# Graph attention and ternary FFN on one core: weight inspection as ScalarE sums during attention and wo, and a buffer of its own for every piece of the output

## Chip, cores and metric

The kernel runs on one core of one Trainium2 chip. The metric is the device time of one execution in microseconds, as the median of several runs. Lower is better.

## The reference

One layer of graph attention and one feed-forward block act on `x`, 384 nodes by 1024 features in fp32, both with a residual connection.

```
h  = layernorm(x)
q, k, v    = h @ wq.T + bq, h @ wk.T + bk, h @ wv.T + bv           # 1024 -> 1024
q2, k2, v2 = q @ wiq.T + biq, k @ wik.T + bik, v @ wiv.T + biv     # 16 heads of 64
mask[src, dst] = softplus(edge_type_weights)[type - 1], else -inf  # 12288 edges; diagonal filled
x = x + softmax(q2 @ k2.T / 8 + mask) @ v2 @ wo.T + bo
h = layernorm(x)
h = silu((h @ w1.T) * w1_s) * ((h @ w2.T) * w2_s)                  # 1024 -> 512
h = gelu((h @ h1.T) * h1_s);  h = gelu((h @ h2.T) * h2_s)          # 512 -> 512
x = x + (h @ w3.T) * w3_s                                          # 512 -> 1024
```

The five weight matrices of the feed-forward block (w1, w2, h1, h2, w3) hold only -1, 0 and 1 in these inputs.

## The kernel before

**Tiling.** The 384 nodes are three row tiles of 128 (`NT`), the 1024 features eight column tiles (`KF`). Weights come as halves of 2 MB from a pool of four buffers (`load_w`, `prefetch`), on SP's DMA queue in order; the FFN's weights in the rounded type fp32r come on POOL's queue.

**Order.** SP, ScalarE (ACT), VectorE (DVE) and TensorE run in the order in which the code is written. The stages follow one another: layernorm and transposes; the projections q, q2, v, v2, k (`project`, L143 and L152); attention; the product with wo (L423) with its layernorm; the FFN. In the first half POOL scatters the mask's 12288 values into a table in HBM with indirect DMAs (L353) and reads the table back as `nmask`.

**Attention.** There are 24 units (eight pairs of heads by three row tiles) in 13 slots: one unit in the first and the last slot, two in each other. A slot computes the scores on TensorE (`sc`, L460), adds the mask and takes the minimum on DVE (L474), and takes the exps with their sums on ACT (L476). Then it transposes the attention weights of the slot before on TensorE (`pp`, L492), which one copy on DVE (L530) and one on ACT (L531) evict, and normalises its own on DVE (L482, L484). The rest of the k2 projection (L444) is spread over the slots. After every third unit of a pair `weighted` computes the pair's output (L501) and ACT copies it into `aT` (L504).

**The inspection.** The FFN has two branches. The fast one multiplies in fp32r and is exact only when the weights need few mantissa bits; the exact one uses fp32. The kernel decides on the chip. `inspect` loads the weights in 16 pieces of 512 KB (`raw`) on SP's queue, and DVE ORs both halves of each piece into `bits` (L182), two instructions a piece. Eight pieces are looked at in k (through the two `stage` buffers), two at the end of attention plus three in a "trio" buffer of tag "t" ahead of wo, and three more in wo after row tile 0. `gather_bits` then folds the 512 columns to one by nine halving ORs (L592), masks the low 12 bits (L593) and converts (L595). In row tile 2 a matmul with `ones` sums this over the partitions (`fl`, L607), DVE copies it to the integer `flag` (L609), the engines load it into a register (`values_load`, L613), and they branch on it at the FFN (`rest`).

**wo and its layernorm.** For each row tile and half, `multiply_out` finishes an accumulation on TensorE, and `add_out` adds it to `xs` (L584) and takes its statistics (L113) on DVE. `layernorm` takes the aggregate (L122), a square root on ACT (`sd`, L124), the scales (L126, L128) and normalises one half on DVE (L134) and one on ACT (L136). `transpose_x2` (L572) turns a normalised row tile through PSUM into `x2`, with a cast on ACT (L574) and a subtraction on DVE (L565). That of row tile 0 stands behind row tile 1's layernorm, and that of tile 1 between tile 2's two halves, behind the `fl` matmul.

**The output.** The last product (L644) gives seven pieces: five of 128x512 and two of 128x256. DVE multiplies each by the scale (L725) and adds the residual (L726), and SP sends it to HBM (L727). A piece lives in one of the two buffers of tag "stage".

**The tag "t".** It has two buffers, which are taken in turn by qT, vT, kT, pTa, the trios of `raw`, and the FFN's hidden layers `g`.

Of the kernel before, what the change touches and what calls it, by code (L numbers as in the profile page):

```python
# [8 lines left out]
FP = mybir.dt.float32  # L9
FR = mybir.dt.float32r  # L10
BF = mybir.dt.bfloat16
HF = mybir.dt.float16
I32 = mybir.dt.int32
AF = mybir.ActivationFunctionType
ALU = mybir.AluOpType

N = 384
F = 1024
FH = 512
# [3 lines left out]
P = 128  # L23
NT = N // P
# [16 lines left out]
def gnn_ffn_kernel(ctx: ExitStack, tc: tile.TileContext, x, edges, etw, vecs, rows,  # L41
# [4 lines left out]
    nc = tc.nc  # L46
# [14 lines left out]
    xs = act.tile([P, NT, F], FP, name="xs")  # L61
# [103 lines left out]
    def prefetch(between=None):  # L165
        if plan:
# [2 lines left out]
    prefetch(load_small)  # L169


    bits = const.tile([P, FH], I32, name="bits")
    pieces = [(w, i) for w in (w1, w2, h1, h2, w3)
              for i in range(w.shape[0] * w.shape[1] // (P * F))]

    def inspect(raws):
        for raw in raws:
            w, i = pieces.pop(0)
            nc.sync.dma_start(raw, bass.AP(tensor=w.tensor, offset=w.offset + i * P * F,
                                           ap=[[F, P], [1, F]]))  # L180
            for h in range(2):
                nc.vector.tensor_tensor(bits, bits, raw[:, h * FH:(h + 1) * FH].bitcast(I32),  # L182
                                        op=ALU.bitwise_or)


    q2T = act.tile([P, KF, N], FP, name="q2T")
# [4 lines left out]
    with tc.tile_pool(name="edge", bufs=1) as ep, tc.tile_pool(name="krow", bufs=2) as krp, \  # L191
# [180 lines left out]
            if c0 in (2 * CHUNK, 5 * CHUNK):  # L372
                prefetch()
        load_rows()
        nc.vector.memset(bits, 0)
        read = nc.gpsimd.dma_start(nmask, cells).ins
        for i in sent[-DEEP:]:
            after(read, i)
# [26 lines left out]
        for t in range(NT):  # L405
            tc.keep_in_program_order(
                nc.gpsimd.tensor_add(xs[:, t, :], xs[:, t, :], row[:, 1, :]))
        inspect([stage.tile([P, F], FP, tag="stage", name="raw") for _ in range(8)])
        kT = project(xT, "kT", vec[:, BK:])


# [21 lines left out]
    with tc.tile_pool(name="attn", bufs=1) as ap, \  # L433
# [85 lines left out]
        for s, new in enumerate(slots):  # L519
# [7 lines left out]
            for i in range(2):  # L527
# [6 lines left out]
                if i == 0:  # L534
# [4 lines left out]
                    if s >= len(slots) - 2:  # L539
# [1 line left out]
                            begun.append((bank(), 0))  # L541
                        ps, k = begun.pop()
                        begun.append((ps, out_steps(ps, 0, 0, k, k + 3)))
        inspect_more(False, 2)
        out_steps(begun[0][0], 0, 0, KF - 2, KF - 1)
        begun = [(begun[0][0], KF - 1), (bank(), KF - 1)]
        out_steps(begun[1][0], 0, 1, 0, KF - 2)
# [36 lines left out]
        nc.vector.tensor_add(xs[:, t, c], ps, xs[:, t, c])  # L584
        statistics(t, st, half)

    def gather_bits():

        n = FH
        while n > 1:  # L590
            n //= 2
            nc.vector.tensor_tensor(bits[:, :n], bits[:, :n], bits[:, n:2 * n], op=ALU.bitwise_or)  # L592
        nc.vector.tensor_single_scalar(bits[:, 0:1], bits[:, 0:1], 0xFFF, op=ALU.bitwise_and)  # L593
        bitf = small.tile([P, 1], FP, name="bitf")
        nc.vector.tensor_copy(bitf, bits[:, 0:1])  # L595
        return bitf


    inspect_more(True)
    for t in range(NT):  # L600
        st = small.tile([P, 2, 6], FP, name="st")
        add_out(multiply_out(t, 0), t, 0, st)
        if t == 1:
            bitf = gather_bits()
        elif t == 2:
            fl = ps_mm.tile([P, 512], FP, tag="mm", name="fl")
            nc.tensor.matmul(fl[:1, :1], lhsT=bitf, rhs=ones, start=True, stop=True)  # L607
            flag = const.tile([1, 1], I32, name="flag")
            nc.vector.tensor_copy(flag, fl[:1, :1])  # L609
            transpose_x2(1)  # L610
        ps = multiply_out(t, 1)
        if t == 2:
            low_bits = nc.values_load(flag[0:1, 0:1], min_val=0, max_val=P * 0xFFF)  # L613
        add_out(ps, t, 1, st)
        layernorm(t, xn[:, t, :], st)
        if t == 0:
            inspect_more(True)
            assert not pieces
        elif t == 1:
            transpose_x2(0)  # L620


    def rest(fast):

        parts = range(2 if fast else 1)

        def mm_T(ps, todo, o, rows):

            for n, (w, x, k) in enumerate(todo):
                nc.tensor.matmul(ps[:, rows], lhsT=w[:, k, o * P:(o + 1) * P], rhs=x[:, k, rows],  # L632
                                 start=n == 0, stop=n == len(todo) - 1)

        def products(w, src):
            return [(w, src[i], k) for i in parts for k in range(w.shape[1])]

        def accumulate(groups, nk):

            for k in range(nk):  # L640
                for ps, operands in groups:
                    for i in parts:
                        l, r = operands(i, k)
                        nc.tensor.matmul(ps, lhsT=l, rhs=r, start=(i, k) == (0, 0),  # L644
                                         stop=(i, k) == (len(parts) - 1, nk - 1))

        taken = []

        def bank():
            taken.append(len(taken) % 3)  # L650
            if taken[-1] == 2:
                return ps_mm.tile([P, 512], FP, tag="mm", name="ps")
            return ps_ff.tile([P, 512], FP, tag="ff", name="ps")

        if not fast:
            plan.extend(ffn)
            for _ in ffn:
                prefetch()
            (w1s,), (w2s,), h12, (w3s,) = [queue.pop(0) for _ in ffn]
            transpose_x2(NT - 1)  # L660
            x2T = [act.tile([P, KF, N], FP, tag="xT", name="x2T")]
            nc.vector.tensor_add(x2T[0], x2[0].bitcast(FP), x2[1].bitcast(FP))
        else:
            (w1s,), (w2s,) = early
            h12, (w3s,) = [load_w(*p, rounded=True) for p in ffn[2:]]
            x2T = x2

        def hidden():
            a = act.tile([P, KF, N], FR if fast else FP, tag="t", name="g", bufs=2)
            return [a[:, i * KH:(i + 1) * KH, :] for i in parts]  # L670

        g = hidden()

        order_ff = [(o, w) for o in range(KH) for w in (w1s, w2s)]
        ahead = {}
        if fast:
            two, one = slice(0, 2 * P), slice(2 * P, N)
            for n, (o, w) in enumerate(order_ff[:3]):
                if n == 2:
                    transpose_x2(NT - 1)  # L680
                ahead[o, id(w)] = bank()
                mm_T(ahead[o, id(w)], products(w, x2T), o, two)
        for o in range(KH):
            ps = []
            for w in (w1s, w2s):
                p = ahead.get((o, id(w)))
                if p is None:
                    p = bank()
                    mm_T(p, products(w, x2T), o, slice(0, N))
                else:  # L690
                    mm_T(p, products(w, x2T), o, one)
                ps.append(p[:, :N])
            sl = stage.tile([P, N], FP, tag="sl", name="sl")
            nc.scalar.activation(sl, ps[0], AF.Silu, scale=vec[:, W1S + o:W1S + o + 1])
            full = stage.tile([P, N], FP, tag="gf", name="gf") if fast else g[0][:, o, :]
            nc.vector.scalar_tensor_tensor(full, ps[1], vec[:, W2S + o:W2S + o + 1], sl,
                                           op0=ALU.mult, op1=ALU.mult)
            if fast:
                nc.scalar.copy(g[0][:, o, :], full)
                remainder(g[1][:, o, :], full, g[0][:, o, :])  # L700

        for w, s in zip(h12, (H1S, H2S)):
            g2 = hidden()
            for some in (range(3), range(3, KH)):
                ps = [(bank()[:, :N], lambda i, k, o=o: (w[:, k, o * P:(o + 1) * P], g[i][:, k, :]))
                      for o in some]
                accumulate(ps, KH)
                for o, (p, _) in zip(some, ps):
                    full = stage.tile([P, N], FP, tag="gf", name="gf") if fast else g2[0][:, o, :]
                    nc.scalar.activation(full, p, AF.Gelu, scale=vec[:, s + o:s + o + 1])  # L710
                    if fast:
                        nc.vector.tensor_copy(g2[0][:, o, :], full)
                        remainder(g2[1][:, o, :], full, g2[0][:, o, :])
            g = g2
        half = FH // 2
        ends = [(t, a, a + FH) for t in range(NT) for a in (0, FH)][:-1]
        ends += [(NT - 1, FH, FH + half), (NT - 1, FH + half, F)]
        for some in (ends[:3], *([e] for e in ends[3:])):
            ps = [(bank()[:, :b - a], lambda i, k, t=t, a=a, b=b: (
                g[i][:, k, t * P:(t + 1) * P], w3s[:, k, a:b])) for t, a, b in some]  # L720
            accumulate(ps, KH)
            for (t, a, b), (p, _) in zip(some, ps):
                y = stage.tile([P, FH], FP, tag="stage", name="y")
                n = b - a
                nc.vector.tensor_mul(y[:, :n], p, row[:, 2, a:b])  # L725
                nc.vector.tensor_add(y[:, :n], y[:, :n], xs[:, t, a:b])  # L726
                nc.sync.dma_start(out[t * P:(t + 1) * P, a:b], y[:, :n])  # L727

    with tc.If(low_bits == 0, preferred_fallthrough_block=True) as exact:
        rest(True)  # L730
# [36 lines left out]
```

## Time and profile before

| | us |
|---|---|
| median of 3 runs (417.29 to 417.43) | 417.33 |
| the profiled execution | 417.94 |
| its span in the profile | 416.2 |
| TensorE (PE) busy | 401.9 |
| VectorE busy | 175.9 |
| ScalarE busy | 97.4 |
| GpSimd (POOL) busy | 110.3 |
| `bits` ORs of L182 (32 x 691 ns) | 22.1 |

The span is the time from the first to the last thing in the trace of one execution; the execution takes 1.74 us more than its span. Busy times are read by engine: an engine with idle time can take more work, if the idle time lies where the work is put. Stretches of the run: k from 178 to 220 us, attention from 235 to about 316, wo to 358, the FFN's first layer to 384, then its two hidden layers to 396 and the last product with the output from 396 to the end. Rows of a timeline give start, duration, engine, line, operation, what it writes and reads and, in brackets, how long the engine had been idle and what ended that.

### The profile page before, as it was taken

How to read it: one execution, taken by the hardware profiler on the slowest of the kernel's cores; microseconds unless marked ns; L12 is line 12 of the kernel's file. 1: busy time of each engine (PE TensorE's matmuls, PEld its weight loads, DVE VectorE, ACT ScalarE, POOL GpSimd, SP SyncE). 2: the span in 40 equal slices, each digit the busy share in tenths (PEclk: the TensorE clock that was granted, in tenths of full speed). 3: DMA queues.
4: the chain of work that ended last, by engine and by line, in shares of the span. 5: the costliest groups of instructions: out<-in, count | busy, mean ns of one | idle time of the engine just before them, and what ended most of it. 6: DMA issues, size and time to landing. Idle time of an engine off the chain costs nothing.

```text
span 416.2 us, 4309 instructions
## 1 busy us (share of the span) xinstructions
PE 401.9 (97%) x1549; PEld 243.2 (58%) x1549; DVE 175.9 (42%) x567; ACT 97.4 (23%) x217; POOL 110.3 (27%) x117
## 2 busy tenths in 40 slices
PE   7899999999999999999999999999999999999991
PEld 6555555555555444455555555555544444799881
DVE  5646859800000001005500177676764487321464
ACT  4511111111111000001112255655651213221410
POOL 3022435323647374744453710000000000200000
PEclk9999999999999999999999999999999999999996
DMA  7699665899050606075727242000094000740012
GB/s 269 213 334 261 200 217 149 306 388 337 2 202 1 202 2 202 0 259 198 254 100 284 77 112 90 2 0 2 2 354 152 0 0 2 240 165 0 2 50 104
DMA packets 29207, 59.64 MB, mean 143 GB/s; under 512 B 4384, under 2 KB 7296, under 8 KB 29056
## 3 DMA queue, kind: packets, MB, share of 16 engines
q1 hardware_dynamic: 22016, 49.89, 35.5%
q0 software_dynamic: 6880, 9.03, 7.6%
q10 hardware_dynamic: 288, 0.41, 0.3%
q8 instruction: 14, 0.23, 0.2%
q14 instruction: 9, 0.07, 0.1%
HBM read 57.06 MB, written 2.26 MB: 143 GB/s over the span
## 4 chain that ended last, share of the span: by engine, by line
PE 87%; DVE 6%; DMA 3%; ACT 2%; issue 1%; SPq 0%; DVEq 0%; ACTq 0%
PE ps L143 40%; PE ps L152 10%; PE ps L444 10%; PE ps L423 6%; PE ps L632 6%; PE av L501 4%; PE sc L460 4%; PE pp L492 4%; PE ps L644 3%; DMA out<-y 2%; DMA xs<-in_x 1%; DVE st L113 1%; DVE bits L182 1%; DVE y L725 1%; DVE xs L584 1%
## 5 line engine op out<-in xcount | busy, mean ns | idle before, releaser
L353 POOL DMA_INDIRECT tab<-val,cell x96 | 94.8, 987 | 126.3 <-DMA tab<-val,cell 82.8
L337 DVE SCALAR_TENSOR_TENSOR jk<-kr,key,later 128x256 bf16<-128x256 f32 x96 | 39.9, 480 | 16.6 <-DMA kr<-keyd 16.6
L444 PE MATMUL ps<-kT,wik 128*128 128x384 f32 x128 | 43.4, 487 | 0.0
L402 DVE TENSOR_TENSOR v<-ps,row 128x512 f32<-128x512 f32 x6 | 4.2, 692 | 92.4 <-PE ps L152 92.4
L423 PE MATMUL ps<-wo,aT 128*128 128x512 f32 x96 | 42.5, 593 | 0.0
L143 PE MATMUL ps<-xT,wq 128*128 128x384 f32 x128 | 41.5, 487 | 0.3 <-ACT xT L257 0.3
L143 PE MATMUL ps<-qT,wiq 128*128 128x384 f32 x128 | 41.4, 486 | 0.0
L143 PE MATMUL ps<-xT,wv 128*128 128x384 f32 x128 | 41.4, 486 | 0.0
L143 PE MATMUL ps<-xT,wk 128*128 128x384 f32 x128 | 41.4, 486 | 0.0
L152 PE MATMUL ps<-wiv,vT 128*128 128x512 f32 x96 | 41.4, 592 | 0.0
L474 DVE CUSTOM_DVE_ANT_0 e<-sc,nmask 128x384 f32<-128x384 f32 x48 | 23.9, 553 | 31.1 <-PE sc L460 31.1
L143 PEld LDWEIGHTS ps<-xT,wk 128*128 128x128 f32 x128 | 24.3, 190 | 17.2 <-issue 0.5
L143 PEld LDWEIGHTS ps<-xT,wq 128*128 128x128 f32 x128 | 24.2, 190 | 17.2 <-ACT xT L257 0.5
L143 PEld LDWEIGHTS ps<-qT,wiq 128*128 128x128 f32 x128 | 24.3, 190 | 17.0
L143 PEld LDWEIGHTS ps<-xT,wv 128*128 128x128 f32 x128 | 24.3, 190 | 17.0
L476 ACT ACTIVATE e<-e,lo 128x384 f32<-128x384 f32 x48 | 28.9, 604 | 18.5 <-DVE lo L474 18.5
L444 PEld LDWEIGHTS ps<-kT,wik 128*128 128x128 f32 x128 | 23.5, 190 | 14.6 <-ACT k2T L447 0.5
L152 PEld LDWEIGHTS ps<-wiv,vT 128*128 128x128 f32 x96 | 18.2, 190 | 22.7 <-issue 22.5
L182 DVE TENSOR_TENSOR bits<-bits,raw 128x512 int32<-128x512 int32 x32 | 22.1, 691 | 18.5 <-DMA raw<-in_w 17.7
L423 PEld LDWEIGHTS ps<-wo,aT 128*128 128x128 f32 x96 | 17.7, 190 | 20.2 <-issue 20.2
L632 PE MATMUL ps<-x,w 128*128 128x384 f32 (+2 forms) x176 | 25.8, 306 | 0.0
L632 PEld LDWEIGHTS ps<-x,w 128*128 128x128 f32 x176 | 25.1, 190 | 0.5 <-issue 0.5
(113 smaller groups left out, 353.5 us busy)
## 6 DMA issues: line engine op xcount, KB each, us to landing
kr<-keyd SPq DMA_DIRECT2D x11, 576.0 KB, 6.5
raw<-in_w SPq DMA_DIRECT2D x12, 512.0 KB, 4.5
w<-in_w POOLq DMA_DIRECT2D x3, 2048.0 KB, 10.7
wiq<-in_wiq SPq DMA_DIRECT2D x2, 2048.0 KB, 14.9
wv<-in_wv SPq DMA_DIRECT2D x2, 2048.0 KB, 15.8
wiv<-in_wiv SPq DMA_DIRECT2D x2, 2048.0 KB, 16.1
wk<-in_wk SPq DMA_DIRECT2D x2, 2048.0 KB, 8.5
wik<-in_wik SPq DMA_DIRECT2D x2, 2048.0 KB, 8.1
```

Source lines behind the costliest of these rows:

```text
L143: nc.tensor.matmul(ps[:, :N], lhsT=w[:, k, o * P:(o + 1) * P], rhs=src[:, k, :], start=(k == 0), stop=(k == nk - 1))
L152: nc.tensor.matmul(ps[:, :w.shape[2]], lhsT=src[:, k, t * P:(t + 1) * P], rhs=w[:, k, :], start=(k == 0), stop=(k == nk - 1))
L182: nc.vector.tensor_tensor(bits, bits, raw[:, h * FH:(h + 1) * FH].bitcast(I32), op=ALU.bitwise_or)
L337: nc.vector.scalar_tensor_tensor(jk[:, :w], krf[:, j * P:j * P + w], key[:, c:c + 1], later[:, :w], op0=ALU.is_equal, op1=ALU.mult, accum_ ...
L353: i = nc.gpsimd.indirect_dma_start(out=tab, in_=val[:, c:c + 1], in_offset=None, out_offset=bass.IndirectOffsetOnAxis(ap=cell[:, c:c + 1], ...
L423: nc.tensor.matmul(ps, lhsT=aT[:, k, t * P:(t + 1) * P], rhs=wos[half][:, k, :], start=k == 0, stop=k == KF - 1)
L444: nc.tensor.matmul(ps[:, :N], lhsT=wik[o // 4][:, k, o % 4 * P:(o % 4 + 1) * P], rhs=kT[:, k, :], start=(k == 0), stop=(k == KF - 1))
L460: nc.tensor.matmul(sc[:, :N], lhsT=q2T[r, pair, t * P:(t + 1) * P], rhs=k2T[r, pair, :], start=True, stop=True)
L474: nc.vector.tensor_tensor_reduce(e, sc[:, :N], nmask[:, t, :], 1.0, 3e38, op0=ALU.add, op1=ALU.min, accum_out=lo)
L476: nc.scalar.activation(e, e, AF.Exp, bias=lo, scale=-1.0, accum_out=dens[u][:, j:j + 1])
L492: nc.tensor.transpose(pt[:, m, :], e[:, m * P:(m + 1) * P], ident)
L632: nc.tensor.matmul(ps[:, rows], lhsT=w[:, k, o * P:(o + 1) * P], rhs=x[:, k, rows], start=n == 0, stop=n == len(todo) - 1)
```

## The change

Each inspected piece becomes one ACT instruction. It reads the lower 16 bits of each fp32 word as unsigned integers, copies them to a `junk` tile (bf16, one buffer) and writes their sum to a column of `lows`. No piece is looked at in k: six are taken at the ends of the attention slots 1, 3, 5, 7, 9 and 10 (through the two `stage` buffers), three ahead of wo (a trio), four after row tile 0 (a trio and one `stage` piece), and three after row tile 1's layernorm and row tile 0's transposes. `gather_bits` goes: DVE takes the maximum over the 16 columns of `lows` and its minimum with 1 (`any_low`), and the `fl` matmul sums that instead. With no piece in k, the loads of wo on SP's queue are no longer behind eight pieces.

The output pieces are written to slices of one tile `y` of tag "t", so that no two share memory. TensorE's and POOL's instructions stay in their order.

```diff
-    bits = const.tile([P, FH], I32, name="bits")
+    lows = const.tile([P, len(pieces)], FP, name="lows")

     def inspect(raws):
         for raw in raws:
+            at = lows.shape[1] - len(pieces)
             w, i = pieces.pop(0)
             nc.sync.dma_start(raw, bass.AP(tensor=w.tensor, offset=w.offset + i * P * F,
                                            ap=[[F, P], [1, F]]))
-            for h in range(2):
-                nc.vector.tensor_tensor(bits, bits, raw[:, h * FH:(h + 1) * FH].bitcast(I32),
-                                        op=ALU.bitwise_or)
+            low = raw.bitcast(U16).rearrange("p (f two) -> p f two", two=2)[:, :, 0]
+            junk = stage.tile([P, F], BF, tag="junk", name="junk", bufs=1)
+            nc.scalar.activation(junk, low, AF.Copy, accum_out=lows[:, at:at + 1])
...
-        nc.vector.memset(bits, 0)
...
-        inspect([stage.tile([P, F], FP, tag="stage", name="raw") for _ in range(8)])
         kT = project(xT, "kT", vec[:, BK:])
...
-        inspect_more(False, 2)
+            if s in (1, 3, 5, 7, 9, 10):
+                inspect_more(False, 1)
...
-    def gather_bits():
...
         add_out(multiply_out(t, 0), t, 0, st)
-        if t == 1:
-            bitf = gather_bits()
-        elif t == 2:
+        if t == 2:
             fl = ps_mm.tile([P, 512], FP, tag="mm", name="fl")
-            nc.tensor.matmul(fl[:1, :1], lhsT=bitf, rhs=ones, start=True, stop=True)
+            nc.tensor.matmul(fl[:1, :1], lhsT=any_low, rhs=ones, start=True, stop=True)
...
         layernorm(t, xn[:, t, :], st)
         if t == 0:
+            inspect_more(True, 1)
+        elif t == 1:
+            transpose_x2(0)
             inspect_more(True)
             assert not pieces
-        elif t == 1:
-            transpose_x2(0)
+            any_low = small.tile([P, 1], FP, name="any_low")
+            nc.vector.tensor_reduce(any_low, lows, axis=mybir.AxisListType.X, op=ALU.max)
+            nc.vector.tensor_scalar(any_low, any_low, 1.0, None, op0=ALU.min)
...
+        y = act.tile([P, NT, F], FP, tag="t", name="y", bufs=2)
...
-                y = stage.tile([P, FH], FP, tag="stage", name="y")
-                n = b - a
-                nc.vector.tensor_mul(y[:, :n], p, row[:, 2, a:b])
-                nc.vector.tensor_add(y[:, :n], y[:, :n], xs[:, t, a:b])
-                nc.sync.dma_start(out[t * P:(t + 1) * P, a:b], y[:, :n])
+                nc.vector.tensor_mul(y[:, t, a:b], p, row[:, 2, a:b])
+                nc.vector.tensor_add(y[:, t, a:b], y[:, t, a:b], xs[:, t, a:b])
+                nc.sync.dma_start(out[t * P:(t + 1) * P, a:b], y[:, t, a:b])
```

More of the change, by code (lines that the diff above doesn't have):

```diff
@@ L13 @@
 I32 = mybir.dt.int32
+U16 = mybir.dt.uint16
 AF = mybir.ActivationFunctionType
@@ L585, in add_out @@
         statistics(t, st, half)
-    def gather_bits():
[L589 to L596, printed above, removed]
     inspect_more(True)
@@ L612, in gnn_ffn_kernel @@
         if t == 2:
-            low_bits = nc.values_load(flag[0:1, 0:1], min_val=0, max_val=P * 0xFFF)
+            low_bits = nc.values_load(flag[0:1, 0:1], min_val=0, max_val=P)
         add_out(ps, t, 1, st)
```

## The prediction

> **What bounds the kernel now.** I read the busy shares on the page first.
>
> ```profile
> PE 401.9 (97%) x1549; PEld 243.2 (58%) x1549; DVE 175.9 (42%) x567; ACT 97.4 (23%) x217; POOL 110.3 (27%) x117
> ```
>
> TensorE works for 401.9 of 416.2 us, so an edit on VectorE (DVE) or ScalarE (ACT) is worth only what it does to the 14 us in which TensorE stands still. The table by stretches (columns: us, PE, PEld, DVE, ACT, POOL busy, clock, DMA share, GB/s) says where they are.
>
> ```profile
> 235.00:306.00 71.00, 70.65 (x364) 39.86 (x364) 50.10 (x174) 41.93 (x123) 4.83 (x4) 1.00 0.17 49
> 306.00:330.00 24.00, 24.00 (x93) 11.46 (x92) 12.94 (x28) 4.89 (x13) 0.00 (x0) 1.00 0.50 163
> 330.00:350.00 20.00, 19.69 (x54) 8.89 (x52) 14.18 (x35) 4.60 (x8) 0.00 (x0) 1.00 0.00 0
> 396.00:407.10 11.10, 11.10 (x57) 9.31 (x55) 7.55 (x13) 0.96 (x2) 0.00 (x0) 1.00 0.18 68
> 407.10:416.20 9.10, 0.01 (x1) 0.00 (x0) 2.99 (x6) 0.00 (x0) 0.00 (x0) 0.60 0.27 94
> ```
>
> In attention and wo, TensorE misses 0.35 us at 301.4 and 0.34 us at 350.0. The stretch after 407.10 has no TensorE work at all: 9.1 us, and DVE is busy in only 3.0 of them. The chain of waits (start, us, what) shows why.
>
> ```profile
> 402.15 2.01 DMA out<-y
> ...
> 404.26 0.70 DVE y L725
> 404.98 0.70 DVE y L726
> 405.70 2.80 DMA out<-y
> ...
> 408.60 0.70 DVE y L725
> ...
> 410.04 2.05 DMA out<-y
> ...
> 412.18 0.44 DVE y L725
> ```
>
> Each multiplication into `y` waits until the piece two before it has landed in HBM, because the two `stage` buffers take turns. The query on tile `y` gives DVE 3.8 us of such waits, three times. The second place is one row on TensorE, and the third the idle time of ACT (bracket: idle before the row, and who ended it).
>
> ```profile
> 349.50 0.19 PE L607 MATMUL fl<-ones,bitf 128*1 128x1 f32 x2
> 350.03 1.25 PE L572 MATMUL pt<-ident,xn 128*128 128x128 f32 x8 [0.34 <-DVE x L565]
> ```
>
> ```profile
> 271.77 0.61 ACT L476 ACTIVATE e<-e,lo 128x384 f32<-128x384 f32 x1 [1.18 <-DVE lo L474]
> 336.37 0.29 ACT L124 ACTIVATE sd<-mv,eps 128x1 f32<-128x1 f32 x1 [4.92 <-DVE mv L122]
> 347.18 0.29 ACT L124 ACTIVATE sd<-mv,eps 128x1 f32<-128x1 f32 x1 [9.22 <-DVE mv L122]
> ```
>
> **What the Trainium skill says.** "ScalarE: Activation LUTs", section "What ACT_TABLE_LOAD costs": an ACTIVATE takes 186 ns + 0.833 ns per element, about 93 ns more for each per-partition pointer, and neighbours overlap by about 93 ns. The trace agrees: exp over 384 elements with one pointer should be 599 ns and shows 604; xn over 512 with two should be 799 and shows 814. The same page, "Table sets: the hidden batching unit", says that copy is in every set; the built order of the changed kernel has no added table load. "DMA: Bandwidth & Descriptors", "Latency and other measured facts", speaks of a fixed cost of about 2 us per DMA; here 256 KB of output land in 2.0 us and 128 KB in 1.9, so the landing is nearly all latency, which overlaps once nobody waits for it.
>
> **Part 1, the output in its own buffer.** `y` takes the activation buffer of tag "t" that the g before last held; its readers (the h2 matmuls) end at 395.9, before the first y. In the built order all seven multiplications now wait for TensorE alone. Without the waits DVE goes piece after piece: from 400.71 to 402.04 is 1.33 us a piece (the trace's own pair that did not wait). Five pieces start at 400.71, 402.04, 403.37, 404.70, 406.03; the first half piece at 407.36 and the second 0.81 us later (0.45 from its multiplication to its addition, 0.36 on to the next), at 408.17, ending at 409.05. TensorE ends at 407.11, so DVE is the bound here and never waits. Before, the last addition ended at 413.07: 4.0 us earlier. What follows it (issue at 413.09, landing, end at 416.2) is 3.1 us and stays, but the last three transfers now lie 0.8 us apart. Of the pieces of before, the one issued at 405.70 with another behind it took 2.80 us, the others about 2.0. I charge 0.2 us of this and bound it by 0 and 0.8. **-3.8 us, from -4.0 to -3.2.**
>
> **Part 2, nothing in k.** 16 ORs (692 ns each, 11.1 us of DVE), a memset of 0.49 us and eight 512 KB loads leave the stretch 178 to 220. TensorE has no wait there: **0**. The loads of wo on SP's queue come 3.6 us earlier for the first (now behind the k matmuls that free its buffer, at 199), and their first reader is at 306. POOL's scatters waited for landings between 185 and 225; with less traffic they and the mask read behind them (issued 230.03, landed 4.3 us later, needed at 236.09) can only be earlier. If that were wrong, 1.8 us of slack is the cover.
>
> **Part 3, six inspections in attention.** Each is one ACTIVATE over 1024 16-bit words with a stride of two, plus an accumulator read. No row shows it. By the skill's price it is an estimate of 1.04 us; the read (186 ns in the exp rows) adds about 0.1 after overlaps, and in a row each waits for the one before (one `junk` buffer), so I use J = 1.15 us a piece. The lower end is 1.04. Upwards, the stride or the integer input could cost up to twice: 2.0. They stand in front of the exps of slots 2, 4, 6, 8, 10 and 11, where ACT idles 1.53, 1.18, 1.18, 1.18, 1.47 and 1.02 us. Five fit; the last delays its exps by 0.13. Behind a waiting inspection would queue the exps, then the copies of the transposes, for which TensorE waits: slack of that copy is about 0.1 us in slot 2 and 0.7 in slot 4, and in slot 10 it is already late by the 0.35 us above. The raws come in time: SP issues number three when the first inspection ends (about 247), used at 270, and so on; nothing else is behind them on SP until the trio at 300. I take **+0.1 us**, from -0.35 (the stall of slot 10 goes) to +0.6.
>
> **Part 4, ten inspections in wo.** Removed from DVE there: 16 ORs (11.1 us) and the tree of `gather_bits` (nine ORs, an AND, a cast, 345.57 - 342.99 = 2.6 us). None of the first ten held TensorE (316 to 328), but the last six and the tree kept the addition of row tile 1's second half until 345.49, though TensorE had it at 341.66. Now it starts at 341.75. On ACT, in order: three inspections from 330.14 to 333.6 and the table load to 334.9, before the 336.37 at which `sd` needs it; then four from 337.87 to 342.5, before `sd` of tile 1, which becomes ready at 343.43 (341.75 plus addition, statistics and aggregate, 1.68 us as in 345.49 to 347.18). From `sd` to the end of tile 0's two casts is 347.18 to 349.73, less 0.09 overlap: the last three start at 345.9 and end at 345.9 + 3J + 0.1 = 349.45. Their raws wait only for the first trio's end (333.6) and some 5 us of landing. A reduction over 16 numbers and a minimum on DVE (about 0.2 each, as the 128x32 and 128x1 rows of L592) and the way to TensorE make 0.49: the flag's matmul starts at 349.94 instead of 349.50. So TensorE waits anew, 0.44 us, for `any_low`. In return the transposes behind it no longer wait for DVE: before they began at 350.03 and took 1.25 with a second wait inside; now 0.17 after the flag's matmul, at 350.11, and 0.87 like the other such row (342.54 - 341.66), to 350.98 against 351.28. **-0.3 us**; with J = 1.04 it is -0.65, with J = 1.5 it is +1.3 (the four then also delay `sd`).
>
> **Sum.** -3.8 + 0 + 0.1 - 0.3 = -4.0 us. The profiled execution took 417.94 us (span 416.2 and 1.74 around it), 0.61 over the median 417.33. So: span 412.2, its execution 413.9, median **413.3**. The rest of ffn is the same instructions, counted at nothing.
>
> **Rivals.** (B) Inspections are somewhat dear, J near 1.5. The chain ACT, `any_low`, flag then costs 1.3 in wo and 0.4 in attention: -2.1, about 415.2. For it: no row has this operand; against: the price fits exp and xn within 15 ns. (C) The output is limited by its transfers: if the last landings stretch as the 2.80 did, or more, the tail gives 2.5 to 3.2: about 414.3. For it the 2.80; against, 256 KB per 1.33 us is under 200 GB/s where this trace shows 388. (D) Slower: the strided words run at half rate, J = 2.0. The first three push `sd` to 337.42, the four end at 346.9, the last three start at 349.4 and end at 355.5, the transposes end at 357.0 instead of 351.28: +5.7, with +1.0 in attention and -3.8 at the end +2.9, or 420.2. It decides from J = 1.75: there the same walk gives +3.2 and +0.5, no change. Against it: the skill's same price for fp32 and bf16. That the change does nothing is out for part 1, since the order shows the waits gone; that the exact branch would be taken is not, but the sum of lower halves of -1, 0, 1 is zero.
>
> **How the numbers follow.** No change means within 0.2%, about 0.8 us, which is what a measurement of this kernel can tell. The main case 0.78 (412.2 to 414.2), B 0.10, C 0.06, D 0.06. Faster are the first three but for 0.02 near J = 1.7: 0.92; same 0.02; slower 0.06. The low end is -4.0 - 0.65 - 0.35, about 412.3, rounded to 412.2; the high end takes in B: 415.6.
>
> **What would show it.** In the profile after: no wait of DVE on `out<-y`, and the last addition about 2 us after TensorE's last matmul; inspections of 1.04 us on ACT; TensorE waiting for `any_low` about 0.4 us before L607's successor; attention within 0.5 us of its 71. The prediction is wrong if an inspection takes over 1.3 us, if exps start more than 0.3 us later than before relative to their scores, or if the last output lands more than 2.5 us after its issue.

## The result, and the profile after

| | before | after |
|---|---|---|
| median, us | 417.38 | 414.49 |
| span of the profiled execution | 416.2 | 412.8 |
| its execution | 417.94 | 414.55 |

The medians are of four executions each. The ratio is 0.9931, with a 95% interval of 0.9914 to 0.9948: 2.9 us faster. The forecast was 413.3, 4.0 us faster, with a range of 412.2 to 415.6.

The profiled execution of before was a long one for its kernel: in later series the spans of the kernel before had medians of 415.7 to 415.9. So the two spans above overstate the gain, and the medians are to be used.

The busy shares of the kernel after:

```profile
PE 402.2 (97%) x1549; PEld 244.0 (59%) x1549; DVE 151.4 (37%) x525; ACT 114.7 (28%) x249; POOL 109.9 (27%) x117
```

DVE lost 24.5 us and ACT gained 17.3 us of work, and TensorE has the same. The table by stretches of the kernel after (columns as before):

```profile
235.00:306.00 71.00, 70.95 (x365) 40.18 (x366) 50.51 (x175) 48.59 (x136) 2.00 (x2) 1.00 0.26 81
306.00:330.00 24.00, 24.00 (x90) 11.25 (x89) 5.79 (x18) 4.91 (x12) 0.00 (x0) 1.00 0.55 178
330.00:350.00 20.00, 19.60 (x57) 9.10 (x56) 9.52 (x21) 15.29 (x27) 0.00 (x0) 1.00 0.23 79
396.00:407.10 11.10, 10.56 (x55) 8.84 (x53) 8.42 (x15) 0.59 (x1) 0.00 (x0) 1.00 0.26 94
407.10:412.80 5.70, 0.00 (x0) 0.00 (x0) 1.30 (x4) 0.00 (x0) 0.00 (x0) 0.80 0.31 102
```

In wo ACT went from 4.6 to 15.3 us and DVE from 14.2 to 9.5. The stretch without TensorE is shorter. The chain at its end (start, us, what) has no DMA in it any more:

```profile
400.15 0.70 DVE y L717
...
405.55 0.61 DVE y L717
406.16 0.02 issue
406.19 0.69 DVE y L718
...
408.04 0.43 DVE y L718
```

DVE works through the seven pieces without a wait and ends at 408.47, 1.9 us after TensorE's last matmul at 406.56. Before it was 413.07 against 407.11, 6.0 us. But then comes what was not expected. The query on tile `y`, here of the kernel after and for its last two sends, gives the time from issue to landing:

```profile
DMA to landing us min/median/max: 2.0/3.0/3.7
...
L719 SPq DMA_DIRECT2D out<-y x1: 332/332/332, 407.7 to 407.7; - x1
DMA to landing us min/median/max: 3.6/3.6/3.6
...
L719 SPq DMA_DIRECT2D out<-y x1: 332/332/332, 408.5 to 408.5; - x1
DMA to landing us min/median/max: 3.1/3.1/3.1
```

Before, these two landed in 1.9 us; this is the last one:

```profile
L727 SPq DMA_DIRECT2D out<-y x1: 333/333/333, 413.1 to 413.1; - x1
DMA to landing us min/median/max: 1.9/1.9/1.9
```

So 1.2 us of the tail's gain is given back at the last landing.

ScalarE's timeline shows the inspections in their places, and TensorE's the new wait:

```profile
257.77 1.06 ACT L186 ACTIVATE junk<-raw 128x1024 bf16<-128x1024 uint16 x1
258.73 0.19 ACT L186 ACTIVATION_READ_ACCUMULATOR junk<-raw 128x1 f32 x1
259.05 0.62 ACT L477 ACTIVATE e<-e,lo 128x384 f32<-128x384 f32 x1
...
343.07 0.30 ACT L125 ACTIVATE sd<-mv,eps 128x1 f32<-128x1 f32 x1 [1.02 <-DVE mv L123]
```

```profile
349.48 0.19 PE L596 MATMUL fl<-ones,any_low 128*1 128x1 f32 x2 [0.40 <-DVE any_low L613]
349.60 1.09 PE L574 MATMUL pt<-ident,xn 128*128 128x128 f32 x8
```

An inspection takes 1.06 us, or 1.18 from start to start in a row (329.55, 330.73 and 331.91 for the three ahead of wo's first `sd`). The `sd` of row tile 1 had 1.0 us of idle time left in front of it. The exps at 259.05 had 0.1, since the inspection's accumulator read ends at 258.92.

### The profile page after: what moved, and what is told of

It is laid out like the page before. It is cut to its first block, busy times and chain, and to the rows that moved or that the text cites. A ratio compares the mean times of both kernels' runs of the same rounds, so it can differ in the third digit from the quotient of the medians.

```text
span 412.8 us, 4295 instructions
## 1 busy us (share of the span) xinstructions
PE 402.2 (97%) x1549; PEld 244.0 (59%) x1549; DVE 151.4 (37%) x525; ACT 114.7 (28%) x249; POOL 109.9 (27%) x117
## 4 chain that ended last, share of the span: by engine, by line
PE 90%; DVE 4%; ACT 3%; DMA 1%; issue 1%; SPq 0%; ACTq 0%
PE ps L144 40%; PE ps L153 10%; PE ps L445 10%; PE ps L424 8%; PE ps L625 6%; PE av L502 4%; PE sc L461 4%; PE pp L493 4%; PE ps L637 3%; DMA xs<-in_x 1%; DVE y L718 1%; DVE y L717 1%; DVE st L114 1%; ACT junk L186 1%; ACT e L477 1%
## 5 line engine op out<-in xcount | busy, mean ns | idle before, releaser
L391 ACT ACTIVATE kT<-ps,vec 128x384 f32<-128x384 f32 x8 | 4.6, 581 | 77.8 <-PE ps L144 77.8
```

## The experiments

Each ran beside the kernel before on the same chip; times are given as medians, with the ratio to the kernel before. The series ran on several chips, and the kernel before had medians of 417.55 to 417.76 in them, against 417.38 beside the kernel after. So differences of less than about 0.4 us between times of different series say nothing.

**1. The output's buffer alone.**

```diff
 # in the kernel before
+        y = act.tile([P, NT, F], FP, tag="t", name="y", bufs=2)
...
+                nc.vector.tensor_mul(y[:, t, a:b], p, row[:, 2, a:b])
+                nc.vector.tensor_add(y[:, t, a:b], y[:, t, a:b], xs[:, t, a:b])
+                nc.sync.dma_start(out[t * P:(t + 1) * P, a:b], y[:, t, a:b])
```

> The kernel before with the output in its own buffer and nothing else. Theory (the whole gain but some 0.6 us is the tail): DVE's last addition comes 2.0 us after TensorE's last matmul instead of 6.0, but the last piece lands 3 us after its issue instead of 1.9, as in the changed kernel: 2.8 us less than before, about 414.6 (measured for the whole change: 2.9 less). Rival (the landings are slow only because the inspection moved something): the last piece lands in about 2 us, and the time is 4.0 less, 413.4.

Measured: 414.79, ratio 0.9933 (0.9920 to 0.9947). The last two pieces landed 3.3 and 2.8 us after their issue. This edit alone gives 2.8 us, and the slow landings come with it, not with the inspection.

**2. The inspection alone.** The kernel after, with `y` back in the `stage` buffers.

> The changed kernel with the output pieces back in the two stage buffers, so the moved inspection alone. Theory: TensorE's last matmul ends 0.55 us earlier than before (0.2 of it at the start, where a second profile also differs, so 0.3 to 0.6), the tail is as before: 416.8 to 417.1. Rival (the inspection carries more of the gain): 416 or less.

Measured: 417.57 against 417.60, ratio 0.9999 (0.9991 to 1.0008). Less than expected: no gain that can be told from nothing. TensorE's last matmul ended at 406.56, as in the kernel after.

**3. Where the landings go: fewer sends.** The DMA queues also carry packets of the kind "instruction". Those of 16 KB took 0.9 to 1.65 us each in these runs. In the kernel after one starts within 0.2 us from 408.6 (columns: packets, MB, share of the time of 16 DMA engines):

```profile
q1 hardware_dynamic: 65, 0.07, 97.2%
q8 instruction: 1, 0.02, 44.0%
```

"Advanced Engine Details and Errata" of the Trainium skill, section "ISA Cache", gives an instruction cache line as 16 KB or 256 instructions; the packets have that size. By their times such a packet starts at 405.01 (1.43 us long), when the slow third piece (3.7 us) is under way, and at 408.68 (1.41 us), with the last two. A packet of 8 KB starts at 409.21, but run 1 has none there, and its last two pieces were late as well. In the kernel before they start at 406.08, where one piece took 2.80 us, and at 409.19, between two pieces.

```diff
+                if (t, a) not in ((1, 0), (1, FH), (2, 0)):
-                nc.sync.dma_start(out[t * P:(t + 1) * P, a:b], y[:, t, a:b])
+                    nc.sync.dma_start(out[t * P:(t + 1) * P, a:b], y[:, t, a:b])
```

> The changed kernel, but three of the seven output pieces (the two of row tile 1 and the first of row tile 2) are computed and never sent, so the DMA engines are nearly idle when the two last half pieces are issued. Theory A (a 16 KB instruction packet, which starts about 2.1 us after TensorE's last matmul and holds one of the DMA engines for 1.4 us, stands in the way of the last rows): the two last pieces still land about 3 us after their issue, and the span shrinks by less than 0.3 us. Theory B (the last pieces queue behind the earlier ones): they land in about 1.9 us, and the span shrinks by about 1.2 us, to 411.6.

Measured, in a single execution: both last pieces landed in 2.5 us, the span was 412.3. Neither theory's numbers were met. With nothing queued in front of them they were still late by 0.6 us; but the packet, too, was shorter (0.95 us from 408.10). This run does not decide.

**4. TensorE's jump later.**

```diff
+        if fast:
+            idle = bank()
+            for i in range(8):
+                nc.tensor.matmul(idle, lhsT=g[0][:, i % KH, :P], rhs=w3s[:, i % KH, :FH], start=i == 0,
+                                 stop=i == 8 - 1)
```

> The changed kernel with eight more matmuls of 512 columns on TensorE after the last product, into a bank that nobody reads; they only make TensorE reach its jump to the end of the program 1.8 us later. Theory A (the instruction packet follows TensorE's jump): the packet starts at about 410.5 instead of 408.7, behind the data of the last pieces; they land about 2.0 us after their issue, and the span is up to 1.1 us shorter, unless the end of TensorE's own program then comes last. Theory B (queueing of transfers): the landings stay at about 3 us and the span at 412.8.

Measured: 415.32, ratio 0.9946 (0.9931 to 0.9961), 0.8 us slower than the kernel after. The packets moved, but by 1.1 us for the first (to 406.11) and 0.7 for the second (to 409.37), not by the 1.8 that I expected, and the second now met the last piece alone. The two last sends of this run:

```profile
L719 SPq DMA_DIRECT2D out<-y x1: 333/333/333, 407.6 to 407.6; - x1
DMA to landing us min/median/max: 2.0/2.0/2.0
...
L719 SPq DMA_DIRECT2D out<-y x1: 332/332/332, 408.4 to 408.4; - x1
DMA to landing us min/median/max: 3.8/3.8/3.8
```

The piece issued at 407.6 has the same sends ahead of it as the one that took 3.6 us in the kernel after, and lands in 2.0. The third piece, too, went from 3.7 to 2.0, since the first packet now started only as it landed (406.11 against 406.18). Delay follows the packet, not the queue. The time missed its mark because the packet moved onto the worst place.

**5. The jump away from the end.** The branch that runs is laid out behind the exact one in the program.

```diff
-    with tc.If(low_bits == 0, preferred_fallthrough_block=True) as exact:
+    with tc.If(low_bits == 0, preferred_fallthrough_block=False) as exact:
```

> The changed kernel with the two branches laid out the other way round in the program: the branch that runs stands behind the exact one, so that the engines jump at its start and have nothing to jump over at its end. Theory A (the packets at the end belong to the jump over the exact branch): the two 16 KB packets in the last 10 us are gone or stand at the branch (350 to 362 us) instead, the last pieces land in about 2.0 us, 1.1 us less at the end; at the branch TensorE may wait 0 to 3 us for its instructions: 413.4 to 416.5. Theory B (the packets come with the number of instructions executed, wherever the jump is): they stay at the end, and so does the landing of 3 us: 414.5 or more.

Measured: 413.41, ratio 0.9901 (0.9886 to 0.9917). From the DMA queues of this run, first in the window from 396.6 us to the end: output alone, and no instruction packet (the last one, of 8 KB, starts at 396.55). Then one line of the window from 350 to 358: three 16 KB packets, where the kernel after has one (at 352.35), so the two of the end stand at the branch instead. Last comes the query on tile `y`.

```profile
q1 hardware_dynamic: 1008, 1.57, 28.8%
```

```profile
q8 instruction: 3, 0.05, 2.6%
```

```profile
DMA to landing us min/median/max: 2.0/2.0/2.0
```

This trace has the landings of three of the seven pieces, 2.0 us each, and that of the last piece is not among them. It can be reckoned from the span, which ends 1.19 us after the last landing in the kernels before and after. Here it ends 3.08 us after the last send, at 408.54, so the last piece landed in 1.9 us, as before; in the kernel after it ends 4.28 us after that send. The time is 1.1 us less than that of the kernel after, as theory A had it. At the branch TensorE did not wait: its matmuls run on from 350.57 through 357.04 without an idle gap.

**6. The inspections doubled.**

```diff
+            for _ in range(2):
-            nc.scalar.activation(junk, low, AF.Copy, accum_out=lows[:, at:at + 1])
+                nc.scalar.activation(junk, low, AF.Copy, accum_out=lows[:, at:at + 1])
```

> The changed kernel with every inspection done twice (the same instruction repeated), so that a piece takes 2 x 1.18 = 2.36 us of ACT. By the walk of the prediction: the first layernorm's square root is delayed by 2.0 us to 337.9, the four inspections behind it end at 348.9, the last three at 358.5, and TensorE waits about 9.8 us for any_low instead of 0.4. In attention each double inspection passes the idle time of its slot by about 1 us, and TensorE stands 1 to 3 us in all. About 425 to 427. Rival (the inspections have more cover than that, and only the last three count): TensorE waits 3.5 us more, 418.

Measured, in a single execution: 428.74. TensorE's wait for `any_low` and its waits in attention, in its timeline:

```profile
250.48 0.55 PE L494 MATMUL pp<-ident,e 128*128 128x128 f32 x3 [0.41 <-ACT pTa L533]
263.56 0.55 PE L494 MATMUL pp<-ident,e 128*128 128x128 f32 x3 [0.34 <-ACT pTb L533]
289.14 1.56 PE L446 MATMUL ps<-kT,wik 128*128 128x384 f32 x4 [0.52 <-ACT aT L506]
303.88 0.55 PE L494 MATMUL pp<-ident,e 128*128 128x128 f32 x3 [0.99 <-ACT pTb L533]
361.58 0.19 PE L597 MATMUL fl<-ones,any_low 128*1 128x1 f32 x2 [9.56 <-DVE any_low L614]
```

The walk gave 9.8 us of wait and the trace shows 9.56; attention stands 2.3 us. The cover of the inspections is as thin as the prediction had it. The time is 1.7 us above the expected 427. The transposes and the product behind the long wait took 1.97 and 8.34 us instead of 1.09 and 7.03, 2.2 us more in all, since TensorE's clock was low there (columns as in the tables by stretches, the clock behind POOL's):

```profile
361.00:364.00 3.00, 2.42 (x11) 2.18 (x12) 2.22 (x6) 1.02 (x4) 0.00 (x0) 0.50 0.03 5
364.00:368.00 4.00, 4.00 (x8) 1.65 (x7) 0.85 (x2) 0.28 (x1) 1.50 (x2) 0.74 0.05 3
```

**7. The flag later.** The `fl` matmul and its copy go behind `transpose_x2(1)`.

```diff
-            fl = ps_mm.tile([P, 512], FP, tag="mm", name="fl")
-            nc.tensor.matmul(fl[:1, :1], lhsT=any_low, rhs=ones, start=True, stop=True)
-            flag = const.tile([1, 1], I32, name="flag")
-            nc.vector.tensor_copy(flag, fl[:1, :1])
             transpose_x2(1)
+            fl = ps_mm.tile([P, 512], FP, tag="mm", name="fl")
...
```

> The changed kernel with the flag's matmul moved behind the transposes of row tile 1, so that TensorE no longer waits for the last inspection there. Theory: the 0.40 us that TensorE waited for any_low goes, the matmul itself then finds its operand ready, and TensorE's last matmul comes 0.4 us earlier: 414.1. Rival: the wait is replaced by another (the transposes wait for the casts or for the layernorm of row tile 1), no change: 414.5.

Measured: 414.26, ratio 0.9926 (0.9912 to 0.9939). The 0.40 us wait is gone from TensorE and its last matmul ends at 406.10 instead of 406.56. In the time it shows as 0.2 us, which is inside the intervals.

**8. POOL adds the first row tile's pieces.**

```diff
-                nc.vector.tensor_add(y[:, t, a:b], y[:, t, a:b], xs[:, t, a:b])
+                adder = nc.gpsimd if t == 0 else nc.vector
+                adder.tensor_add(y[:, t, a:b], y[:, t, a:b], xs[:, t, a:b])
```

> The changed kernel with the residual of the first two output pieces added by POOL instead of DVE. DVE then ends its last addition 0.9 to 1.2 us earlier, about 407.5. Theory A (the second instruction packet, at about 408.7 whatever DVE does, delays only rows that are still on their way then): most rows of the last piece are through before it, so the last landing is 2.0 to 3.0 us after its issue and the gain is 0.3 to 2.0 us: 412.5 to 414.2. Theory B (transfers queue behind each other): the pieces come closer together, the last one lands 3 us or more after its issue, gain 0 to 0.9.

Measured: 414.51, ratio 0.9930 (0.9916 to 0.9943), no gain (the profile is that of the longest of five executions, 415.09). DVE's last addition ended 1.1 us after TensorE's last matmul (407.96 against 406.82), 0.8 us less than in the kernel after. But POOL took 1.29 and 1.73 us for its two pieces and DVE up to 1.01 for additions of 0.69 in the meantime, and so the second to the fourth piece were sent within 1.0 us (404.35 to 405.36) into the first packet (405.53). They landed in 4.0 to 4.4 us and the last in 3.9. The Trainium skill ("SBUF — State Buffer", "Who interferes with whom") says that DVE and GpSimd share a port pair; the longer rows agree. With the eight idle matmuls as well:

> The pieces of row tile 0 added by POOL, and the eight idle matmuls behind the last product that move the second instruction packet from 408.7 to about 409.4. Theory A: all rows of the last piece are through before the packet starts; it lands 2.0 to 2.2 us after its issue at about 407.6, and the span is about 411.0: 412.7. Theory B: as in the run with POOL alone, or slower by what TensorE's later end costs: 413.6 to 415.

Measured: 413.80, ratio 0.9912 (0.9897 to 0.9927); the last piece landed in 2.3 us, with the second packet at 410.47. The time fell 1.1 us short of the mark, and 0.7 of this is that the piece was sent at 408.29 and not at 407.6. DVE had ended its addition at 407.67, but the send before it took 1.29 us on SP instead of 0.33, while the first packet was under way (406.56 to 407.82).

**9. Combinations.** First these two with the flag later:

> The changed kernel with the flag's matmul behind the transposes, the pieces of row tile 0 added by POOL and the eight idle matmuls at the end. If the gains of the separate runs add (0.4 us on TensorE from the first, 0.7 to 0.9 from the other two together): 413.4. If the instruction packets fall otherwise against the output, 413.4 to 414.3.

Measured: 413.55, ratio 0.9906 (0.9891 to 0.9921), near the first case and inside the second. Then sixteen idle matmuls and the flag later, with DVE adding all pieces:

> The changed kernel with the flag's matmul behind the transposes and sixteen idle matmuls at the end, DVE doing all additions. TensorE ends 3.5 us later than its last useful matmul, the first packet comes at about 407, the second at about 410.5. Theory A: the last piece, issued at 408.0, has its rows through between the two packets if the first ends by 408.5 and lands in 2.0 to 2.5 us; 413.5, unless TensorE's own end then comes last. If a packet still meets the last rows: 414.3 to 415.

Measured: 413.94, ratio 0.9910 (0.9896 to 0.9923); packets at 407.21 and 411.25. Here, too, the send before the last took long on SP:

```profile
L719 SPq DMA_DIRECT2D out<-y x1: 1306/1306/1306, 407.6 to 407.6; - x1
```

So the last piece, whose addition ended at 408.41, was sent at 409.05 and not at 408.0. Reckoned from the span as in run 5, it landed in 1.9 us: theory A was right on the landing, and the late send is enough for the 0.4 us by which the time missed 413.5. And last the two edits that stood on their own reasons, the flag later and the branch laid out last:

> The two edits that gained by themselves, together: the flag's matmul behind the transposes of row tile 1 (0.4 us of TensorE's wait for any_low) and the branch that runs laid out behind the exact one (1.1 us at the last landing). If they add: 413.0. If the flag, which now comes 0.4 us later against the jump at the branch, makes TensorE wait for its instructions there: 413.4 or more.

Measured: **412.96**, ratio 0.9886 (0.9869 to 0.9902). The gains add, within what the intervals can tell. This is the fastest version, some 1.5 us under the kernel after.

## Why the prediction came out as it did

**The range held, and partly by luck.** The median of 414.49 lies above the main case (412.2 to 414.2) and beside rival C, which had a chance of 0.06. The range reached up to 415.6 because of rival B, dear inspections, and these did not come. One of the prediction's own signs of being wrong did come: the last output landed 3.1 us after its issue, and it allowed 2.5.

**Part 1, the tail: the mechanism right, one term too small.** The waits on `out<-y` are gone; DVE was the bound with 1.33 us a piece; its lead over before was 4.05 us against TensorE, as worked out. The step that failed is "I charge 0.2 us of this and bound it by 0 and 0.8". The last landing took 3.1 us instead of 1.9, so the term was 1.2, outside its bound, and the tail gave 2.8 (measured alone), not 3.8. I had read the 2.80 us of one piece of before as the price of a transfer behind it. Runs 4 and 5 show that an instruction packet does this, and one started at 406.08, during that piece; in run 5 pieces with others close behind landed in 2.0. The second packet of before fell into a gap between its last pieces. Taking the gap away moved the output onto it. The rival about transfers had the right size (2.5 to 3.2) with the wrong cause.

**Part 2: right.** No piece in k, no change on TensorE. The scatters on POOL were done earlier: its addition to `xs` behind the mask's read began at 214.8 instead of 230.8.

**Part 3: right in kind.** An inspection took 1.06 us, 1.18 in a row (taken: 1.15), and fitted into ACT's idle time: the first exps behind each of the six began within 0.1 us of DVE's result, no later than before. The delay of 0.13 us that I charged for the last one did not come. Slot 10, where TensorE had stood for 0.35 us, is 0.3 us shorter from the start of its k2 matmuls to the next scores (298.66 to 301.91 before, 298.46 to 301.42 after), and so is attention as a whole. I had bounded this side by -0.35 and taken +0.1.

**Part 4: the walk right, the sum 0.2 us too good.** The new wait is 0.40 us against 0.44 worked out. From the start of row tile 2's first half to that of its second it was 8.58 us before (342.54 to 351.12) and 8.48 after (342.05 to 350.53): -0.1 against -0.3. The step that failed is "0.87 like the other such row": that is from start to start, and I set it against the 1.25 of a row's whole length; from start to start the row of before had 1.09.

Parts 3 and 4 together gave TensorE 0.4 us (its last matmul ends at 406.56, and at 406.97 in run 1), where I had 0.2, and the time nothing that could be measured (run 2: between 0.4 us faster and 0.3 slower). Part of it can be lost at the end: in run 2's profile the last piece landed in 2.2 us instead of 1.9, with an 8 KB instruction packet on its way.

**The rival that ends slower** had its place right: with the inspections doubled (J = 2.36), TensorE waits where the walk said and about as long, and the time is 11 us over before. Nothing made a single inspection that dear.

## What to carry to other kernels

When a wait on a landing is taken away at the end of a kernel, the gain is the engine's lead less what the landings become when they no longer have the DMA engines to themselves; look up which other packets, those of the instructions among them, lie in the last microseconds. Look, too, at how a branch is laid out: here the running side stood ahead of the other and had to jump over it at its end, and instruction packets came just when the last output was sent. Laying it out the other way moved them to a place where nobody waited. Work put into another engine's idle time costs nothing only up to that time in each place, so add it up at the place with least: here 0.1 us in front of the exps of attention, against 1.0 us before a square root.

## What the runs showed of the hardware

- Instruction packets of 16 KB took 0.9 to 1.65 us each on the DMA side, and output that met one landed in 2.5 to 4.4 us instead of 2.0 (pieces sent in the last 0.4 us of a packet, or landing in its first 0.4, came nearly in time). That the rows delayed are those on the same DMA engine is argued from the tail of the traffic (16 to 20 GB/s, 1 to 2 packets at a time, from 410.0 to 411.1 in the kernel after), not measured by engine.
- The two packets at the end followed TensorE's program: eight more matmuls moved them by 1.1 and 0.7 us. That is not all, since with POOL adding, and TensorE ending 0.3 us later, they moved by 0.5 and 1.1 us. What fixes the 2.1 to 2.9 us from the first one's end to the second's start stays open.
- In five runs (3, both of 8 and the first two of 9) a send that was issued during such a packet took 0.9 to 1.4 us on SP instead of 0.33, and ended 0.4 us after the packet. Other sends inside a packet did not (0.33 us at 405.58 in the kernel after). What tells them apart stays open.
- With the inspections doubled TensorE had no work from 352.0 to 361.6. Its granted clock fell to 0.50 some 4 us into this pause, stayed there until 366.0, over 4 us after the restart, and stood at 1.00 from 366.5. The Trainium skill ("TensorE: Matmul & The Clock Gate", "Part 1") tells of a half-rate state after idle time; the trace agrees.
- ScalarE took 1.04 to 1.06 us (1041 to 1065 ns, 16 rows) to read 1024 integers of 16 bits with a stride of two elements, where the prediction had estimated 1.04. Against that estimate neither the stride nor the integers show as a cost.
